# Value products of two quads in one run, and a pair of block swaps issued from ScalarE

## The chip, the cores and the metric

One core of one Trainium2 chip runs the whole kernel. The metric is the device time of one execution in microseconds; the kernel before takes 577.23 us, the median of three runs (576.55 to 578.54). TensorE multiplies, VectorE, ScalarE and GpSimd do the elementwise work, SyncE issues DMA transfers from a queue that it works off in order. In the profile the engines are called PE, DVE, ACT, POOL and SP.

## What is computed

A layer norm, a cross attention with 32 heads of width 32, an output projection and a residual, for 8 batches of 256 queries and 256 keys, in 32 bit floats; keys and values are the same context. The reference, cut to what matters:

```python
x = (hidden_states - mu) * rsqrt(var + LN_EPS) * ln_gamma + ln_beta     # (8, 256, 1024)
Q, K, V = split_heads(x @ Wq.T), split_heads(memory_keys), split_heads(memory_values)
scores = einsum('bhsd,bhtd->bhst', Q, K) * scale                        # and the mask
attn = einsum('bhst,bhtd->bhsd', softmax(scores), V)
out = residual + attn.reshape(B, S, 1024) @ Wout.T
```

## The kernel before

The work is cut into quads: four heads (128 columns) of one batch. There are 8 batches of NQ = 8 quads, N = 64 quads in all. A loop over slots n = 0 to 63 writes the program out in the order in which every engine will run it; nothing is reordered later. A slot n on TensorE holds

- `scores(n + 1)` (L486): 8 products with 32 contraction rows, 16 matmuls in the trace because a 32 bit product takes two, into four PSUM tiles;
- `values(n - 2)` (L629): the probabilities of quad n-2 times its values. 32 products, 64 matmuls in the trace, each with 64 contraction rows and 32 output columns; they go to two PSUM tiles `pv`;
- wide products, 128 by 128: steps of the output projection of the batch before (L715, a Strassen scheme with the products A11, A12, S2, S3, A22, S1, S4 and sums S1 to S4 of its operands), and a query product of the next batch but one (L345 in the first batches, L447 later).

Meanwhile `softmax(n + 1)` runs on the other engines. For each of four heads j: VectorE adds the mask and takes the minimum (`exps`, L522), ScalarE exponentiates and sums (L526), VectorE takes a reciprocal (L533), GpSimd scales (`normalize`, L535), VectorE transposes blocks of 32 by 32 into the tile `pT` (`blocks`, L541). Between the exponentials of head 0 and head 1 stands `copy_at`, in which ScalarE copies every finished `pv` out of PSUM (L642).

`pT` has halves 0 and 1 on each of four groups of 32 partitions, and the block transposes leave two of them in the wrong place. They are swapped by DMA. ScalarE first copies half 1 aside into `pc` (`aside`, L547, two calls). Then the first pair of swaps (L607) writes half 0 of the odd groups over half 1 of the even groups, and the second pair (L611) brings the even groups' old half 1, out of `pc`, into half 0 of the odd groups. The second pair therefore waits until the first has landed.

All these transfers go through SyncE's queue. For a slot n it holds, in this order: output stores that stand among the softmax work (L758), the load of the values of quad n (`load_v`, L144, two buffers, so it also waits for the products of quad n-2), the first swaps of quad n+1, loads for later (`between`: keys L136, a weight ring L414, residual L151, input L130), the second swaps of quad n+1, and after the softmax the moves of the transposed input of a later batch (`move_x`, L332), 4 in slot 4 of a batch, 6 in slot 5 and 6 in slot 6, for most batches.

`copy_at` writes into the tiles `at`: one for each half batch, three buffers. The first copy of quad 8b+4 takes the buffer of the first half of batch b-1, which is read for the last time by that batch's sum S1, an addition on GpSimd (`sum_at`, L691).

Of the kernel before, what the change touches and what calls it, by code (L numbers as in the profile page):

```python
# [46 lines left out]
F32 = mybir.dt.float32  # L47
# [4 lines left out]
P = 128  # L52
# [7 lines left out]
def xattn_kernel(  # L60
# [11 lines left out]
    nc = tc.nc  # L72
    B, S, D = x.shape
# [3 lines left out]
    NQ = NC  # L77
    NH = P // HD
    NS = S // P
    NT = T // P  # L80
    NO = D // 512
    K = 32
# [4 lines left out]
    N = B * NQ  # L87
# [16 lines left out]
    ps_v = ctx.enter_context(tc.tile_pool(name="ps_v", bufs=2, space=PS))  # L104
# [366 lines left out]
    mbs, scs, pTs, pvs, ats, pos = {}, {}, {}, {}, {}, {}  # L471
# [21 lines left out]
            pass  # L493

    tails = []


    def softmax_parts(n, copies=(), ahead=(), between=(), hooks={}, fill=()):

        fill = list(fill)

        def fill_in():
            if fill:
                fill.pop(0)()

        pss = scs[n]  # L510
        pT = pTs[n] = ptp.tile([P, 2, NI, NH, NS, K], F32, tag="pT", name=f"pT_{n}")
        pc = asp.tile([P, NI, NH, NS, K], F32, tag="pc", name=f"pc_{n}")
        es, mns, dens = {}, {}, {}

        def exps(j, part=range(NS)):
            if 0 in part:
                es[j] = ep.tile([P, NS, T], F32, tag="e", name=f"e_{n}_{j}")
                mns[j] = sm.tile([P, NS], F32, tag="mn", name=f"mn_{n}_{j}")
                dens[j] = sm.tile([P, NS], F32, tag="den", name=f"den_{n}_{j}")
            e, mn, den = es[j], mns[j], dens[j]  # L520
            for s in part:
                nc.vector.tensor_tensor_reduce(  # L522
                    out=e[:, s, :], in0=pss[j][:, s, :], in1=mbs[n // NQ], scale=1.0,
                    scalar=NO_SCORE, op0=ALU.add, op1=ALU.min, accum_out=mn[:, s : s + 1],
                )
                nc.scalar.activation(  # L526
                    e[:, s, :], e[:, s, :], AF.Exp, bias=mn[:, s : s + 1], scale=-1.0,
                    accum_out=den[:, s : s + 1],
                )

        def normalize(j):
            rden = sm.tile([P, NS], F32, tag="rden", name=f"rden_{n}_{j}")
            nc.vector.reciprocal(rden, dens[j])  # L533
            for s in range(NS):
                nc.gpsimd.tensor_scalar(  # L535
                    es[j][:, s, :], es[j][:, s, :], rden[:, s : s + 1], 1.0,
                    ALU.mult, ALU.mult,
                )

        def blocks(j):  # L540
            nc.vector.transpose(  # L541
                pT[:, :, :, j, :, :].rearrange("p a i s k -> p (a i) s k"),
                es[j].rearrange("p s (b t) -> p b s t", t=K),
            )

        def aside(j):
            nc.scalar.copy(pc[:, :, ts(j, 2)], pT[:, 1, :, ts(j, 2)])  # L547

        if n == 0:
            for j in range(NH - 1):  # L550
                exps(j, (0,))
            yield
            exps(NH - 1, (0,))
            fill_in()
            yield
            for j in range(NH):
                exps(j, (1,))
            normalize(0)
            fill_in()
        else:  # L560
            exps(0)
            while tails:
                tails.pop()()
            late = "p1" in hooks
            if not late:
                for done in list(pvs):
                    copy_at(done)
            exps(1)
            for hook in hooks.get("soon", ()):
                hook()  # L570
            exps(2)
            normalize(0)
            for hook in hooks.get("p1", ()):
                hook()
            exps(3)
            if late:
                for done in list(pvs):
                    copy_at(done)
        if n <= NQ:
            for copy in copies:  # L580
                copy()
        for hook in hooks.get(0, ()):
            hook()
        normalize(1)
        fill_in()
        blocks(0)
        for hook in hooks.get(1, ()):
            hook()
        normalize(2)
        fill_in()  # L590
        blocks(1)
        aside(0)
        normalize(3)
        fill_in()
        blocks(2)
        while fill:
            fill_in()
        if n > NQ:
            for copy in copies:
                copy()  # L600

        def tail():
            blocks(3)
            aside(1)

            for r in range(2):
                nc.sync.dma_start(pT[ts(2 * r, K), 1], pT[ts(2 * r + 1, K), 0])  # L607
            for load in between:
                load()
            for r in range(2):  # L610
                nc.sync.dma_start(pT[ts(2 * r + 1, K), 0], pc[ts(2 * r, K)])  # L611

        for load in ahead:
            load()
        if n < NQ or N - NQ < n < N - 1:
            tails.append(tail)
        else:
            tail()
        yield

    def values(n):
        pvs[n] = [
            ps_v.tile([P, 2, NS, K], F32, tag="pv", name=f"pv_{n}_{r}") for r in range(2)
        ]
        pT = pTs.pop(n)
        for i in range(NI):
            for j in range(NH):
                for r in range(2):
                    nc.tensor.matmul(  # L629
                        pvs[n][r][j * HD : (j + 1) * HD],  # L630
                        vs[n][ts(r, 2 * K), i, ts(j, HD)],
                        pT[ts(r, 2 * K), :, i, j, :, :],
                        start=(i == 0), stop=(i == NI - 1),
                    )

    def copy_at(n):
        b, c = divmod(n, NQ)
        k, c = divmod(c, NK)
        if c == 0:
            ats[b, k] = atp.tile([P, NK, NS, NA, K], F32, tag="at", name=f"at_{b}_{k}")  # L640
        for r, pv in enumerate(pvs.pop(n)):
            nc.scalar.copy(  # L642
                ats[b, k][:, c, :, ts(r, 2), :], pv.rearrange("p a s k -> p s a k")
            )
# [39 lines left out]
    def sum_at(b, name, c=slice(0, NK)):  # L684
        if name == "S2" and c.start == 0:
            s2s[b] = up.tile([P, NK, P], F32, tag="s2", name=f"s2_{b}")
        one, two, op = {
            "S3": ("A11", "A21", ALU.subtract), "S2": ("A22", "S3", ALU.subtract),
            "S1": ("S2", "A11", ALU.add), "S4": ("A12", "S2", ALU.subtract),
        }[name]  # L690
        nc.gpsimd.tensor_tensor(  # L691
            operand(b, name)[:, c], operand(b, one)[:, c], operand(b, two)[:, c], op
        )
# [213 lines left out]
    for b in range(B - 1):  # L907
        done, ends = 0, b == B - 2
        for i, counts in enumerate(steps_of(b)):
            n = NQ * (b + 1) + i  # L910
# [12 lines left out]
            product_steps(*one)  # L923


    for n in range(N):
        b, i = divmod(n - NQ, NQ)
        new_q = new_qs[n]
# [23 lines left out]
        for what, one, *args in evacuations[n]:  # L952
            if one == B - 2:
                now.append(partial(what, one, *args))
            else:
# [1 line left out]
                if one not in P1_ASIDE and i in (1, 2):  # L957
                    place = "p1" if what is keep_p1 else "soon"
                hooks.setdefault(place, []).append(partial(what, one, *args))
        if n >= 2:  # L960
            values(n - 2)
        project_steps(n, 1)
        copies = [partial(copy_q, q) for q in new_q]
# [43 lines left out]
            if n == slot:  # L1007
                sum_at(one, "S3")
        if b >= 0:
            for name in {2: ("S4",), 3 if b == B - 2 else 5: ("S1",)}.get(i, ()):  # L1010
                sum_at(b, name)
            if i == 0 and b == B - 2:
                sum_at(b, "S2", slice(0, NK - 1))
# [44 lines left out]
    for c in range(2):  # L1058
        end_steps(to_c11, "A12", B21, (c,), (0,))
        end_steps(to_c21, "A22", T4, (c,), (0,))  # L1060
    values(N - 2)
    copy_at(N - 2)
    end_sum(slice(2, 3), nc.gpsimd)
# [3 lines left out]
    s2t2 = ps_o.tile([P, 512], F32, tag="po", name="po_end_s2")  # L1067
    end_steps(s2t2, "S2", T2, range(2), (0,))
    values(N - 1)
    copy_at(N - 1)  # L1070
    end_sum(slice(3, 4), nc.vector)
# [66 lines left out]
```

## Time and profile before

| | us |
|---|---|
| median of three runs | 577.23 |
| lowest, highest | 576.55, 578.54 |
| span of the profiled execution | 577.0 |
| TensorE matmuls busy | 567.3 |
| VectorE busy | 460.4 |
| ScalarE busy | 411.7 |
| GpSimd busy | 409.8 |

The span goes from the first to the last instruction of one profiled execution. Busy time counts overlapping instructions once; matmuls are pipelined and their ends are modelled, so the distance from start to start says more than a length. SyncE has no busy time, since it only issues. In a row of the timeline stand start, length, engine, line, operation, tiles, shape and count, and in brackets the idle time of the engine before it with what ended it. "SPq" and "ACTq" are issues of a DMA; the length is that of the issue, and the landing is told in other views.

### The profile page before, as it was taken

What the parts mean: (1) busy time and instruction counts of PE and PEld (TensorE: products, weight loads), DVE (VectorE), ACT (ScalarE), POOL (GpSimd) and SP (SyncE); (2) the same over time, 40 slices, a digit from 0 to 9 for tenths busy, and PEclk for the clock granted to TensorE, in tenths of its full rate; (3) what the DMA queues carried; (4) which work ended last, traced back from release to release, by engine and by line L of the source; (5) the groups of instructions that cost most, each with busy time, mean ns of one, the idle gap of its engine ahead of it and who ended that gap; (6) DMA issues with size and microseconds to landing.
All of it is one profiled execution on the core that took longest, in us unless ns stands there. A gap on an engine that the chain in (4) does not pass through costs nothing. (4 is left out here: it accounts for less than half of the span.)

```text
span 577.0 us, 20128 instructions
## 1 busy us (share of the span) xinstructions
PE 567.3 (98%) x7162; PEld 394.2 (68%) x7162; DVE 460.4 (80%) x1695; ACT 411.7 (71%) x1425; POOL 409.8 (71%) x677
## 2 busy tenths in 40 slices
PE   8999998999999999999999999999999999999997
PEld 8788784667667777677676677667766767755543
DVE  5888887788877879979888788988878878779823
ACT  4697886677667877688677867768767776769810
POOL 1778898889896896876568675676658657448770
PEclk9999999899999999999999999999999999999999
DMA  8974766656677777957678856687567864446751
GB/s 304 394 206 126 208 161 180 192 148 166 185 220 222 200 208 207 271 166 201 188 213 228 211 138 189 212 240 206 148 161 236 224 170 130 130 138 178 199 166 73
DMA packets 50100, 111.69 MB, mean 194 GB/s; under 512 B 9424, under 2 KB 10192, under 8 KB 50000
## 3 DMA queue, kind: packets, MB, share of 16 engines
q1 hardware_dynamic: 49712, 110.40, 66.8%
q8 instruction: 57, 0.93, 0.7%
q14 instruction: 43, 0.35, 0.2%
q10 hardware_dynamic: 288, 0.01, 0.0%
HBM read 60.04 MB, written 10.49 MB: 122 GB/s over the span
## 5 line engine op out<-in xcount | busy, mean ns | idle before, releaser
L535 POOL TENSOR_SCALAR e<-e,rden 128x256 f32<-128x256 f32 x512 | 236.0, 478 | 116.9 <-DVE rden L533 114.4
L526 ACT ACTIVATE e<-e,mn 128x256 f32<-128x256 f32 x512 | 253.9, 501 | 50.7 <-DVE mn L522 49.6
L541 DVE STREAM_TRANSPOSE pT<-e 128x512 f32<-128x512 f32 x256 | 180.9, 707 | 44.7 <-POOL e L535 32.7
L522 DVE CUSTOM_DVE_ANT_0 e<-sc,mb 128x256 f32<-128x256 f32 x512 | 185.4, 416 | 26.4 <-PE sc L486 26.0
L547 ACT COPY pc<-pT 128x512 f32<-128x512 f32 x128 | 79.0, 617 | 72.1 <-DVE pT L541 36.6
L526 ACT ACTIVATION_READ_ACCUMULATOR e<-e,mn 128x1 f32 x512 | 97.9, 191 | 0.0
L345 PE MATMUL pq<-xnT,wq 128*128 128x256 f32 (+1 forms) x368 | 84.1, 383 | 0.6 <-ACT qa L354 0.6
L345 PEld LDWEIGHTS pq<-xnT,wq 128*128 128x128 f32 x368 | 68.9, 190 | 15.4 <-issue 3.7
L629 PE MATMUL pv<-pT,v 64*32 64x128 f32 x4096 | 74.7, 274 | 3.5 <-DMA v<-in_kv_dram 2.9
L629 PEld LDWEIGHTS pv<-pT,v 64*32 64x32 f32 x4096 | 57.5, 105 | 26.7 <-issue 14.7
L486 PEld LDWEIGHTS sc<-k,qa 32*128 32x128 f32 x1024 | 46.2, 184 | 41.9 <-issue 23.6
L715 PE MATMUL po_S<-wo,at 128*128 128x512 f32 x152 | 74.3, 606 | 0.0
L486 PE MATMUL sc<-k,qa 32*128 32x256 f32 x1024 | 73.6, 401 | 0.1
L715 PE MATMUL po_A<-wo,at 128*128 128x512 f32 x128 | 61.2, 620 | 0.3 <-ACT qa L354 0.3
L715 PE MATMUL po_S<-wo,s 128*128 128x512 f32 x104 | 49.9, 606 | 0.0
L533 DVE RECIPROCAL rden<-den 128x2 f32<-128x2 f32 x256 | 37.6, 147 | 7.7 <-ACT e L526 6.8
L522 DVE DVE_READ_ACCUMULATOR2_ANT mn<- 128x1 f32 x512 | 42.5, 83 | 0.0
L715 PEld LDWEIGHTS po_A<-wo,at 128*128 128x128 f32 x128 | 23.4, 193 | 26.2 <-issue 24.5
L447 PEld LDWEIGHTS pq_A<-xnT,wq 128*128 128x128 f32 x320 | 37.3, 192 | 4.8 <-issue 3.6
L715 PEld LDWEIGHTS po_S<-wo,at 128*128 128x128 f32 x152 | 25.8, 190 | 19.7 <-issue 19.1
L447 PE MATMUL pq_A<-xnT,wq 128*128 128x128 f32 x320 | 37.3, 275 | 0.0
L748 POOL TENSOR_TENSOR r<-r,p 128x512 f32<-128x512 f32 x23 | 29.4, 1278 | 7.1 <-DMA r<-in_x_dram 3.3
(96 smaller groups left out, 608.7 us busy)
## 6 DMA issues: line engine op xcount, KB each, us to landing
v<-in_kv_dram SPq DMA_DIRECT2D x64, 256.0 KB, 3.9
pT<-pT SPq DMA_DIRECT2D x128, 128.0 KB, 3.1
pT<-pc SPq DMA_DIRECT2D x128, 128.0 KB, 3.5
ring<-kept_T SPq DMA_DIRECT2D x18, 512.0 KB, 5.2
k<-in_kv_dram SPq DMA_DIRECT2D x32, 256.0 KB, 3.1
x<-in_x_dram SPq DMA_DIRECT2D x14, 512.0 KB, 5.1
r<-in_x_dram SPq DMA_DIRECT2D x28, 256.0 KB, 5.1
out_dram<-r SPq DMA_DIRECT2D x28, 256.0 KB, 3.0
```

Source lines behind the costliest of these rows:

```text
L345: nc.tensor.matmul(pqs[n], wq[:, o, c, :], xnTs[b](c), start=(c == 0), stop=(c == NC - 1),)
L447: nc.tensor.matmul(pqs[b][:, o, :], w[:, c], x_[:, c], start=begins and o + c == 0, stop=c == NK - 1, skip_group_check=True,)
L486: nc.tensor.matmul(scs[n][j][:, s, :], qa[r, n % NQ, ts(s, P)], ks[n - n % 2][r, n % 2, :], start=True, stop=True,)
L522: nc.vector.tensor_tensor_reduce(out=e[:, s, :], in0=pss[j][:, s, :], in1=mbs[n // NQ], scale=1.0, scalar=NO_SCORE, op0=ALU.add, op1=ALU.m ...
L526: nc.scalar.activation(e[:, s, :], e[:, s, :], AF.Exp, bias=mn[:, s : s + 1], scale=-1.0, accum_out=den[:, s : s + 1],)
L533: nc.vector.reciprocal(rden, dens[j])
L535: nc.gpsimd.tensor_scalar(es[j][:, s, :], es[j][:, s, :], rden[:, s : s + 1], 1.0, ALU.mult, ALU.mult,)
L541: nc.vector.transpose(pT[:, :, :, j, :, :].rearrange("p a i s k -> p (a i) s k"), es[j].rearrange("p s (b t) -> p b s t", t=K),)
L547: nc.scalar.copy(pc[:, :, ts(j, 2)], pT[:, 1, :, ts(j, 2)])
L629: nc.tensor.matmul(pvs[n][r][j * HD : (j + 1) * HD], vs[n][ts(r, 2 * K), i, ts(j, HD)], pT[ts(r, 2 * K), :, i, j, :, :], start=(i == 0), s ...
L715: nc.tensor.matmul(po, operand(b, name)[:, c], wo[:, which, c], start=begins and c == 0, stop=c == NK - 1, skip_group_check=not begins,)
L748: nc.gpsimd.tensor_tensor(r, r, p1s[b], ALU.add)
```

## The change

Three things change.

1. `values_pair(n)` writes the value products of quads n and n+1 one behind the other, into two PSUM tiles that hold both quads. The slots in `PAIRS`, odd ones from 11 to 55 without those of residue 1 modulo 8, call it for quads n-2 and n-1; the slot behind a paired one has no value products. The two quads' copies then both stand in the paired slot's softmax.
2. In the softmax of quads 10 to 56 the first pair of block swaps is issued by ScalarE, behind its second copy aside, and no longer by SyncE. The second pair stays where it was.
3. The sum S1 of a batch moves from slot 5 to slot 4 of the following batch (not in the last ones, where it is in slot 3 as before).

```diff
+    BY_ACT = range(NQ + 2, N - NQ + 1)
...
+            queue = nc.scalar if n in BY_ACT else nc.sync
             for r in range(2):
-                nc.sync.dma_start(pT[ts(2 * r, K), 1], pT[ts(2 * r + 1, K), 0])
+                queue.dma_start(pT[ts(2 * r, K), 1], pT[ts(2 * r + 1, K), 0])
...
-    def values(n):
-        pvs[n] = [
+    def values_pair(n):
+        both = [
+            ps_v.tile([P, 2, 2, NS, K], F32, tag="pv", name=f"pv_{n}_{r}") for r in range(2)
+        ]
+        for i in range(2):
+            values(n + i, [tile_[:, i] for tile_ in both])
+
+    def values(n, to=None):
+        pvs[n] = to or [
             ps_v.tile([P, 2, NS, K], F32, tag="pv", name=f"pv_{n}_{r}") for r in range(2)
         ]
...
+    PAIRS = [n for n in range(NQ + 3, N - NQ, 2) if n % NQ != 1]
+
...
-        if n >= 2:
+        if n in PAIRS:
+            values_pair(n - 2)
+        elif n >= 2 and n - 1 not in PAIRS:
             values(n - 2)
...
-            for name in {2: ("S4",), 3 if b == B - 2 else 5: ("S1",)}.get(i, ()):
+            for name in {2: ("S4",), 3 if b == B - 2 else 4: ("S1",)}.get(i, ()):
```

## The prediction

> **What bounds the kernel now.** I read the page first, then the stages, then the timeline engine by engine.
>
> ```profile
> span 577.0 us, 20128 instructions
> PE 567.3 (98%) x7162; PEld 394.2 (68%) x7162; DVE 460.4 (80%) x1695; ACT 411.7 (71%) x1425; POOL 409.8 (71%) x677
> 233.05:300.98 67.93, 67.93 (x922) 48.06 (x921) 58.22 (x213) 51.30 (x179) 46.00 (x81) 1.00 0.73 205
> ```
>
> The third line is one batch in the middle (eight slots) from the view by stages; its columns are length, PE, PEld, DVE, ACT, POOL, granted clock, DMA share and GB/s. TensorE has no idle there, so a microsecond less of TensorE work is a microsecond of time, and a stall of TensorE is lost in full. The other engines have room, but each serves the quads one after another, so their latency counts. The span of 577.0 us stands at the median of the runs, 577.23 us; sums are made on 577.0.
>
> TensorE's order in a slot n is: scores of quad n+1, value products of quad n-2, then wide products. One slot, from the timeline (start, length of the merged row):
>
> ```profile
> 249.93 1.15 PE L486 MATMUL sc<-k,qa 32*128 32x256 f32 x16
> 251.00 0.89 PEld L629 LDWEIGHTS pv<-pT,v 64*32 64x32 f32 x64 [0.33 <-issue]
> 251.01 1.16 PE L629 MATMUL pv<-pT,v 64*32 64x128 f32 x64
> 252.09 1.98 PE L715 MATMUL po_S<-wo,s 128*128 128x512 f32 x4
> ```
>
> Start to start, scores take 1.08 us and a run of values 1.08 us. The 64 weight loads of the run fill only 0.89 us, at 14 ns each; the other 0.19 us is the change of tile shape behind the run.
>
> **Part 1: values in pairs.** The list of odd slots comes out with 18 entries, residues 3, 5 and 7 of each batch of 8. An odd slot gets 128 matmuls of one shape, the even slot behind it none. Saved is one shape change per pair: 18 x 0.19 = 3.4 us. In the even slot, wide products now follow the scores directly. Early in the trace that pair of shapes stands too:
>
> ```profile
> 22.55 1.15 PE L486 MATMUL sc<-k,qa 32*128 32x256 f32 x16
> 23.62 1.14 PE L345 MATMUL pq<-xnT,wq 128*128 128x257 f32 x4
> ```
>
> Scores before wide products take the same 1.07 us, so the saving is not given back there. **Term: -3.4 us** (bounds -3.4 and 0).
>
> What the pairing asks for: the values of an even quad n run in slot n+1 and no longer in slot n+2. Its value tile v and its four block swaps must land about 7.6 us sooner. The load of v is issued in slot n, on the sync queue, behind everything queued before it. For quad 30 (scores at 267.80) the queue did this:
>
> ```profile
> 276.77 1.14 SPq L607 DMA_DIRECT2D pT<-pT  x2
> 277.96 0.58 SPq L130 DMA_DIRECT2D x<-in_x_dram  x1
> 279.10 1.14 SPq L611 DMA_DIRECT2D pT<-pc  x2
> 280.29 4.41 SPq L332 DMA_DIRECT2D xnT<-xe  x6
> 284.80 0.53 SPq L758 DMA_DIRECT2D out_dram<-r  x1
> 285.42 0.41 SPq L144 DMA_DIRECT2D v<-in_kv_dram  x1
> v<-in_kv_dram SPq DMA_DIRECT2D x64, 256.0 KB, 3.9
> ```
>
> The last line is from the page: a v load lands 3.9 us (median) after issue, so this one lands at 285.42 + 3.9 = 289.3. The order of these entries is the same after the change, except that the first swaps leave the queue. They were not late here, and the second swaps (L611) wait for their landing whoever issued them; then come six moves at 0.7 us each, an output store, and only then v. When is it wanted? Slot 31 begins with its scores:
>
> ```profile
> 284.82 1.15 PE L486 MATMUL sc<-k,qa 32*128 32x256 f32 x16
> 145.56 1.15 PE L486 MATMUL sc<-k,qa 32*128 32x256 f32 x16
> 147.00 0.40 SPq L144 DMA_DIRECT2D v<-in_kv_dram  x1
> 421.70 1.15 PE L486 MATMUL sc<-k,qa 32*128 32x256 f32 x16
> 423.40 0.41 SPq L144 DMA_DIRECT2D v<-in_kv_dram  x1
> ```
>
> The second run of a pair begins 1.08 + 0.89 = 1.97 us behind the scores; and the slot itself begins 0.2 us sooner (the pair slot before it 0.89 longer, the even one 1.08 shorter). Quad 30: 284.82 + 1.97 - 0.2 = 286.6, short by 2.7 us. The other pairs of rows are the first and the last of the five quads with six moves ahead of v (14, 22, 30, 38, 46): 147.00 + 3.9 = 150.9 against 147.3, short by 3.6; and 427.3 against 423.5, short by 3.8. Mean 3.4. **Term: five times 3.4 = +17 us.** Nothing hides it: the next instructions of TensorE are queued behind these values. ScalarE's copies of both value tiles stand between the first and second head's exponentials and wait for the whole pair, so the next softmax is held for as long and gains no lead. Bounds: from above 5 x 3.8 = 19 us; from below the quickest landings, of v 2.8 us in this answer for its line and of the swaps 1.1 us under their median (part 2), which leave 5 x (3.4 - 1.1 - 1.1) = 6 us.
>
> ```profile
> L144 SPq DMA_DIRECT2D v<-in_kv_dram x48: 376/532/1725, 97.8 to 496.1; - x48
> DMA to landing us min/median/max: 2.8/4.0/6.8
> ```
>
>
> The quads of residue 2 (10, 18, 26, 34, 42, 50) are paired in slots 11 to 51; the first and the last of the six:
>
> ```profile
> 109.08 0.41 SPq L144 DMA_DIRECT2D v<-in_kv_dram  x1
> 109.43 1.15 PE L486 MATMUL sc<-k,qa 32*128 32x256 f32 x16
> 454.34 0.40 SPq L144 DMA_DIRECT2D v<-in_kv_dram  x1
> 454.74 1.15 PE L486 MATMUL sc<-k,qa 32*128 32x256 f32 x16
> ```
>
> Short by 109.08 + 3.9 - 109.43 - 1.97 = 1.6 us and by 1.5. Some of these lie behind a queue that the change relieves, so I take two thirds of 6 x 1.55: **+6 us** (bounds 0 and 9). Residue 4:
>
> ```profile
> 266.07 0.53 SPq L144 DMA_DIRECT2D v<-in_kv_dram  x1
> 267.80 1.15 PE L486 MATMUL sc<-k,qa 32*128 32x256 f32 x16
> ```
>
> 269.97 against 269.57: at the edge. I take 0 (bounds 0 and 6 x 0.4 = 2.4).
>
> **Part 2: two swaps on ScalarE.** Neither an issue between computing instructions of ScalarE nor its own price there stands in the trace; the nearest rows are its two issues at the start and the pair on the sync queue, 1.14 above.
>
> ```profile
> 0.72 0.41 ACTq L195 DMA_DIRECT2D gam<-in_gamma_dram  x1
> 1.16 0.45 ACTq L196 DMA_DIRECT2D bet<-in_beta_dram  x1
> 268.06 0.64 ACT L547 COPY pc<-pT 128x512 f32<-128x512 f32 x1
> 269.56 0.51 ACT L526 ACTIVATE e<-e,mn 128x256 f32<-128x256 f32 x1 [0.86 <-DVE mn L522]
> 252.12 1.24 ACT L252 ACTIVATE x<-x,shift,rstd 128x1024 f32<-128x1024 f32 x1
> ```
>
> So 0.9 to 1.14 us per quad; I take 1.1, since these are the same transfers. They wait for the copy aside and stand ahead of the next quad's exponentials. ScalarE idled 0.86 us at that point, so 0.25 us shows in an ordinary slot. Behind an even slot, whose successor's scores come 1.08 us sooner, up to 1.3 us shows; and where a normalization (the 1.24 us row, two per batch) stands there, all 1.1. What is late next: the exponentials, the last transpose, the swaps, and v behind them. I take 0.5 us on each of the eleven late loads: **+5.5 us** (bounds 0 and 11 x 1.1 = 12).
>
> The gain it could bring is an earlier landing of the first swaps:
>
> ```profile
> L607 SPq DMA_DIRECT2D pT<-pT x96: 507/582/1892, 98.4 to 499.6; - x96
> DMA to landing us min/median/max: 2.2/3.3/5.6
> ```
>
> For quad 30 the second swaps went out at 279.10, 2.3 us behind the first swaps' issue: nothing is left to win there. [...]
>
> **Part 3: the sum S1** goes from slot 5 of a batch to slot 4 on GpSimd, because the copies of the pair reach the buffer that it frees one slot sooner. It is the same addition beside the same softmax work, a slot in which GpSimd then has two, and the next slot one: 0 (bounds 0 and one addition, 1.3 us by the row of its like below, in six batches = 8, if it came late for those copies).
>
> ```profile
> 251.02 1.29 POOL L691 TENSOR_TENSOR at<-at,s 128x512 f32<-128x512 f32 x1
> ```
>
> **What a stall sets off.** In the one place where the values already waited for v, the clock fell:
>
> ```profile
> 101.18 1.25 PE L629 MATMUL pv<-pT,v 64*32 64x128 f32 x64 [2.05 <-DMA v<-in_kv_dram]
> 102.36 3.68 PE L715 MATMUL po_A<-wo,at 128*128 128x512 f32 x4
> 102.48:105.88 3.40, 3.40 (x5) 1.34 (x6) 2.75 (x17) 3.03 (x13) 3.39 (x4) 0.50 0.81 216
> ```
>
> After 2.05 us of waiting, 3.4 us ran at clock 0.50, which costs 1.7 us. The five long stalls are longer than that one; I take three such falls: **+5 us** (bounds 0 and 5 x 1.7 = 8.5). [...]
>
> Sum: 577.0 - 3.4 + 17 + 6 + 5.5 + 5 = **607 us**.
>
> **Rivals.**
> - *ScalarE paces the batch, and the loads come in time.* From the first exponential (269.56) to the end of the copy aside (the swap issue at 276.77) a quad takes 7.2 us; with 1.1 behind it 8.3, eight of them plus two normalizations 68.9 us, against 67.93 - 3 x 0.19 = 67.4 for TensorE. The batch would be 1.0 us longer than now, 5.75 batches: 583 us. With the short stalls of the lower bound (6) it is 589. For it: swaps that overtake the sync queue. Against it: six moves and the store stay ahead of v. It decides where 8.3 us passes the mean slot.
> - *Faster:* the loads come in time and ScalarE's slack covers the issues: 577 - 3.4 = 573.6. For it: TensorE alone is full today. Against it: the walk of quad 30.
> - *Worse:* full clock falls (8.5), issue delay (12), late residues 2 and 4 (9 + 2.4) and 19 for the five: 577 - 3.4 + 50 = 624.
> - *The pairing does nothing* (no shape change saved) and nothing stalls: 577.
>
> **How the numbers follow.** Late loads as summed, 595 to 620: 0.55. ScalarE or short stalls, 580 to 595: 0.22. Worse, over 620: 0.10. Faster: 0.09. No change: 0.04. A measurement of this kernel tells some 0.3% (1.7 us) from none. Predicted 607; the range 585 to 624 leaves out faster and no change (0.13), a little of the ScalarE case and the far end (0.07 together). Slower 0.87, same 0.04, faster 0.09.
>
> **What would show it.** In slots 15, 23, 31, 39 and 47 a wait of values for v or for the swaps of 3 us or more, each; some 2 us or less in slots of residue 3; runs of 128 value matmuls with no gap elsewhere, 0.9 us longer than 64; clock 0.50 behind the long waits; the first exponential 0.3 to 1.3 us later behind its scores. Wrong it would be if the v loads of even quads leave the sync queue 3 us earlier than they did, or if TensorE stays without idle through a batch.

## The result and the profile after

The changed kernel takes 638.47 us, the median of four runs (635.44 to 639.66), against 577.1 us for the kernel before on the same chip (four runs, 576.55 to 578.54). The ratio is 1.1045, with a 95% interval of 1.1007 to 1.1084. The forecast was 607, with a range up to 624: the sign was right, and the time lies above the range. In the experiments below, runs more than 1.5% above the fastest run of the same kernel are left out of the times. (In the code after, the values are at L638, the first swaps at L609, the second at L613, the exponentials at L527, the copy aside at L548, the projection's steps at L724, the output store at L767; the other lines named here have kept their numbers.)

First the page of the kernel after:

```profile
span 637.3 us, 19999 instructions
PE 584.5 (92%) x7162; PEld 403.5 (63%) x7162; DVE 462.3 (73%) x1695; ACT 413.3 (65%) x1425; POOL 410.2 (64%) x677
```

The span grew by 60.3 us. TensorE's busy time grew by 584.5 - 567.3 = 17.2, its idle time from 577.0 - 567.3 = 9.7 to 637.3 - 584.5 = 52.8, by 43.1. The other engines do the same work as before in a longer time. So there are two questions: what did TensorE wait for, and why was it busy for longer with the same 7162 matmuls? The view of the waits answers the first (line, releaser, total us, times, longest):

```profile
PE pv L638 <- DMA v<-in_kv_dram: 23.7, 9, 4.7
PE pv L638 <- issue: 16.0, 6, 7.0
PE po_S L724 <- DVE r L766: 5.1, 8, 1.3
PE po_S L724 <- issue: 1.6, 1, 1.6
```

Waits in front of value products make up 23.7 + 16.0 = 39.7 us. In the kernel before the same view had

```profile
PE pv L629 <- DMA v<-in_kv_dram: 2.9, 2, 2.1
PE pv L629 <- DMA pT<-pT: 0.5, 1, 0.5
```

so 36.3 us are new. "issue" is the name the view gives where it sees no releaser; for the longest of these, 7.0 us, the timelines below show a load of v landing there. The last two rows, 6.7 us, are projection steps that wait for VectorE to empty their PSUM tile. 36.3 + 6.7 = 43.0 is the whole new idle time.

The view by stretches answers the second. The columns are the stretch and its length, the busy times of PE, PEld, DVE, ACT and POOL, the granted clock, the DMA share and GB/s. The first row is the batch of quads 26 to 33, which took 67.93 before; the others are the stretches at half clock.

```profile
255.33:335.28 79.95, 70.24 (x921) 49.38 (x921) 58.53 (x212) 51.68 (x180) 46.04 (x81) 0.96 0.63 176
...
111.50:118.20 6.70, 5.68 (x69) 3.27 (x70) 2.17 (x13) 5.58 (x20) 2.10 (x3) 0.50 0.66 190
155.90:162.50 6.60, 5.51 (x70) 3.84 (x71) 1.70 (x7) 3.36 (x15) 1.52 (x4) 0.50 0.90 229
237.80:244.40 6.60, 5.95 (x76) 4.54 (x77) 2.06 (x7) 3.70 (x16) 1.73 (x5) 0.50 0.54 143
316.30:323.00 6.70, 3.28 (x66) 2.41 (x67) 0.00 (x0) 1.13 (x6) 0.00 (x0) 0.50 0.93 239
398.30:401.50 3.20, 3.20 (x66) 2.23 (x64) 0.00 (x0) 1.28 (x7) 0.00 (x0) 0.50 0.92 276
476.80:480.00 3.20, 3.20 (x61) 1.93 (x44) 0.00 (x0) 1.62 (x8) 0.00 (x0) 0.50 0.45 104
514.30:517.50 3.20, 3.20 (x66) 2.29 (x65) 0.90 (x5) 1.56 (x9) 0.93 (x2) 0.50 0.85 258
```

In these seven rows, which are cut up to 0.2 us inside the stretches, TensorE was busy at half clock for 30.0 us; half of that, 15.0, is lost, against 1.7 before: 13 us more. That leaves 17.2 - 13 = some 4 us of the busy time, and the 2.5 us that the pairing saves besides, that no row of these views names.

Now quad 30, the one that the prediction walked through. On the sync queue and on ScalarE (start, length of the issue):

```profile
302.40 0.58 SPq L144 DMA_DIRECT2D v<-in_kv_dram  x1
303.03 0.47 SPq L130 DMA_DIRECT2D x<-in_x_dram  x1
309.05 1.15 SPq L613 DMA_DIRECT2D pT<-pc  x2
310.25 3.99 SPq L332 DMA_DIRECT2D xnT<-xe  x6
314.34 0.54 SPq L767 DMA_DIRECT2D out_dram<-r  x1
314.97 0.40 SPq L144 DMA_DIRECT2D v<-in_kv_dram  x1
```

```profile
303.62 1.16 ACTq L609 DMA_DIRECT2D pT<-pT  x2
```

And on TensorE, the paired slot 31 with its wait, and a pair without one two slots earlier:

```profile
293.72 2.10 PE L638 MATMUL pv<-pT,v 64*32 64x128 f32 x128
295.75 1.12 PE L724 MATMUL po_S<-wo,at 128*128 128x512 f32 x2
...
310.33 1.26 PE L486 MATMUL sc<-k,qa 32*128 32x256 f32 x16
311.53 1.16 PE L638 MATMUL pv<-pT,v 64*32 64x128 f32 x64
319.72 2.08 PE L638 MATMUL pv<-pT,v 64*32 64x128 f32 x64 [7.04 <-issue]
```

The load of v goes out at 314.97, behind second swaps, six moves and a store, as forecast. It lands at 319.63 by the transfer's record, and the second run of the pair starts at 319.72, after 7.04 us of idle where 2.7 were forecast. The rest of the slip stands in the rows ahead: the second swaps left 309.05 - 303.62 = 5.4 us after the first swaps' issue, where before it was 2.3. The x load, formerly behind the first swaps, now stood right ahead of them; that it made the difference is likely, but no run was made for it.

In the pair without a wait, 2.03 us pass from the start of the values to the start of the projection step; one run alone takes 1.09. So a second run costs 0.94 and saves 1.09 in the next slot: about 0.14 us per pair, not 0.19.

### The profile page after: what moved, and what is told of

The parts are those of the page before. It is cut to its first block, busy times and chain, and to the rows that moved or that the text cites. A ratio compares the mean times of both kernels' runs of the same rounds, so it can differ in the third digit from the quotient of the medians.

```text
span 637.3 us, 19999 instructions
## 1 busy us (share of the span) xinstructions
PE 584.5 (92%) x7162; PEld 403.5 (63%) x7162; DVE 462.3 (73%) x1695; ACT 413.3 (65%) x1425; POOL 410.2 (64%) x677
## 4 chain that ended last, share of the span: by engine, by line
PE 38%; POOL 17%; DVE 13%; ACT 11%; DMA 11%; issue 6%; ACTq 3%; SPq 2%; DVEq 0%; POOLq 0%
POOL e L536 13%; PE po_S L724 8%; PE pq L345 6%; ACT e L527 6%; PE pq_A L447 5%; PE pv L638 5%; DVE pT L542 5%; PE sc L486 4%; DMA v<-in_kv_dram 4%; DVE e L523 4%; DMA pT<-pT 3%; ACTq L609 3%; PE po_A L724 3%; PE po_end L791 2%; ACT pc L548 2%
## 5 line engine op out<-in xcount | busy, mean ns | idle before, releaser
L527 ACT ACTIVATE e<-e,mn 128x256 f32<-128x256 f32 x512 | 253.6, 501 | 70.0 <-DVE mn L523 53.4
L548 ACT COPY pc<-pT 128x512 f32<-128x512 f32 x128 | 79.0, 618 | 70.1 <-DVE pT L542 37.4
L638 PE MATMUL pv<-pT,v 64*32 64x128 f32 x4096 | 80.9, 289 | 39.9 <-DMA v<-in_kv_dram 23.7
L638 PEld LDWEIGHTS pv<-pT,v 64*32 64x32 f32 x4096 | 63.5, 111 | 60.7 <-issue 44.7
L527 ACT ACTIVATION_READ_ACCUMULATOR e<-e,mn 128x1 f32 x512 | 98.2, 192 | 0.0
L724 PE MATMUL po_S<-wo,at 128*128 128x512 f32 x152 | 74.3, 606 | 0.0
L486 PEld LDWEIGHTS sc<-k,qa 32*128 32x128 f32 x1024 | 45.7, 184 | 43.1 <-issue 26.1
L724 PE MATMUL po_S<-wo,s 128*128 128x512 f32 x104 | 57.7, 685 | 6.8 <-DVE r L766 5.1
L724 PE MATMUL po_A<-wo,at 128*128 128x512 f32 x128 | 59.5, 605 | 0.3 <-ACT qa L354 0.3
L651 ACT COPY at<-pv 128x128 f32<-128x128 f32 x128 | 25.0, 262 | 35.0 <-PE pv L638 35.0
L724 PEld LDWEIGHTS po_S<-wo,at 128*128 128x128 f32 x152 | 25.8, 190 | 21.4 <-issue 20.9
L724 PEld LDWEIGHTS po_A<-wo,at 128*128 128x128 f32 x128 | 22.9, 189 | 25.7 <-issue 24.0
L724 PEld LDWEIGHTS po_S<-wo,s 128*128 128x128 f32 x104 | 19.9, 212 | 27.7 <-issue 20.5
```

The lines of the kernel that those rows point to most:

```text
L486: nc.tensor.matmul(scs[n][j][:, s, :], qa[r, n % NQ, ts(s, P)], ks[n - n % 2][r, n % 2, :], start=True, stop=True,)
L527: nc.scalar.activation(e[:, s, :], e[:, s, :], AF.Exp, bias=mn[:, s : s + 1], scale=-1.0, accum_out=den[:, s : s + 1],)
L638: nc.tensor.matmul(pvs[n][r][j * HD : (j + 1) * HD], vs[n][ts(r, 2 * K), i, ts(j, HD)], pT[ts(r, 2 * K), :, i, j, :, :], start=(i == 0), s ...
L651: nc.scalar.copy(ats[b, k][:, c, :, ts(r, 2), :], pv.rearrange("p a s k -> p s a k"))
L724: nc.tensor.matmul(po, operand(b, name)[:, c], wo[:, which, c], start=begins and c == 0, stop=c == NK - 1, skip_group_check=not begins,)
```

## The experiments

The theory behind the first experiments was that of the prediction: late loads of v in the paired slots make up most of the loss, and the issues on ScalarE matter only through them. The rival was that ScalarE's issues lengthen the softmax by themselves and pace the batch.

**Pairs alone.** The change with all swaps on the sync queue.

```diff
-    BY_ACT = range(NQ + 2, N - NQ + 1)
+    BY_ACT = ()
```

> The changed kernel with all first swaps back on SyncE; pairs and the moved sum S1 stay. Theory (late loads): the loads of v still stand behind the second swaps and the moves, so the pairs wait: 17 us in slots of residue 7, up to 9 in residue 3, some 12 of half clock behind them, 2.5 saved: 605 to 615 us. Rival (ScalarE's issues are the main cost): pairs alone cost little, under 590 us.

Measured: 610.34 us (609.81 to 615.26), ratio 1.0603 (1.0556 to 1.0651). The page's span and TensorE row, then the view of the waits:

```profile
span 608.5 us, 20095 instructions
PE 577.4 (95%) x7162; PEld 401.1 (66%) x7162; DVE 458.5 (75%) x1695; ACT 413.5 (68%) x1425; POOL 411.3 (68%) x677
```

```profile
PE pv L638 <- issue: 16.0, 8, 3.5
PE pv L638 <- DMA v<-in_kv_dram: 9.0, 5, 3.8
...
PE pv L638 <- DMA pT<-pT: 1.0, 1, 1.0
```

Waits for values are 26.0 us, 22.6 more than before. By slots, from starts of scores, 16.8 of it stands in the five slots of residue 7 and 6.2 in those of residue 3. No projection step waits for VectorE. TensorE was busy at half clock in five stretches (three of 3.4 us, two of 6.8), which costs 9.2 us more than before. With the 2.5 us that 18 pairs save, that makes 577.0 + 22.6 + 9.2 - 2.5 = 606, 2 us short of the span. So the late loads are real, and their waits have the forecast size (22.6 us against 17 + 6). Pairs alone cost 610.3 us against 576.1 of the kernel before beside them: 34 of the 61 us, and no more.

**Swaps alone.** The kernel before with the first swaps of quads 10 to 56 issued by ScalarE.

```diff
+            queue = nc.scalar if n in BY_ACT else nc.sync
...
-                nc.sync.dma_start(pT[ts(2 * r, K), 1], pT[ts(2 * r + 1, K), 0])
+                queue.dma_start(pT[ts(2 * r, K), 1], pT[ts(2 * r + 1, K), 0])
```

> The kernel before with the first swaps of quads 10 to 56 issued by ScalarE, nothing else. Theory (late loads): values are wanted two slots behind their softmax as before, ScalarE's 1.16 us per quad still fit into the mean slot of 8.4 us: 577 to 584 us and no wait for v. Rival (ScalarE's issues): 600 us or more.

Measured: 601.5 us (599.37 to 603.35), ratio 1.043 (1.0393 to 1.0467); the span is 597.4. This is where the forecast fell: 25 us more than the 576.1 of the kernel before beside it, with no pair in the kernel. The view by stretches for the batch of quads 26 to 33, the waits of TensorE, and one end of a softmax on ScalarE (the next quad's first exponential is the last row):

```profile
237.61:312.67 75.06, 69.27 (x922) 48.28 (x921) 58.05 (x210) 50.27 (x174) 45.27 (x79) 1.00 0.66 182
```

```profile
PE po_S L717 <- DVE r L759: 12.9, 13, 2.6
```

```profile
362.34 0.62 ACT L548 COPY pc<-pT 128x512 f32<-128x512 f32 x1 [1.56 <-DVE pT L542]
362.99 1.16 ACTq L609 DMA_DIRECT2D pT<-pT  x2
364.25 0.51 ACT L527 ACTIVATE e<-e,mn 128x256 f32<-128x256 f32 x1 [1.29 <-DVE mn L523]
```

The clock stays at 1.00 and only some 3 us of waits stand in front of value products, as before. Instead the batch takes 75.06 us, 7.1 more (it is the one hit hardest; the six batches from quad 10 on are 21.3 us longer together, by the starts of their scores), and TensorE waits for VectorE's evacuation of the projection, which VectorE does among its softmax work. The exponential starts 0.10 us behind the end of the issue; the wait for `mn` in its bracket counts the issue as idle time, since issues are not counted as work. So the issue stood in the way.

Whether TensorE or the softmax sets the pace shows in another row of the waits: VectorE, which opens a softmax by adding the mask to the scores, waits for TensorE's scores. The first row is of the kernel before, the second of swaps alone:

```profile
DVE e L522 <- PE sc L486: 26.0, 28, 2.1
DVE e L523 <- PE sc L486: 5.8, 12, 1.5
```

Before, the softmax waited for TensorE for 26.0 us; now it hardly does (5.8 us), and TensorE waits for the softmax's engines.

The place of the loss shows in the loop that a softmax forms. The table gives means over quads 10 to 55, from the starts and ends of ScalarE's rows: the body, from a quad's first exponential to the end of its copy aside; the gap from there to the next quad's first exponential; and their sum.

| kernel | body | gap | loop |
|---|---|---|---|
| before | 7.63 | 1.03 | 8.65 |
| pairs alone | 8.34 | 0.99 | 9.33 |
| swaps alone | 7.25 | 1.88 | 9.13 |
| filler on ScalarE (below) | 7.30 | 1.69 | 8.99 |
| after | 8.22 | 1.76 | 9.98 |

Before, the loop is as long as TensorE's slot, because TensorE sets it: the body is stretched by waiting. With the issues the body shrinks to 7.25, its least here, and body and gap together still come to 9.13. That is 0.48 us more than a slot, in 46 quads 22 us. This sum is the lost time told again, since the loops of the quads add up to the time that they take; what the table adds is where it went: the gap grew by 0.85 and the body could give up only 0.38 of it. With the turn of the waits above, the softmax loop has become the bound, most of all where the slots were shortest. In the kernels with pairs the body is long again, because quads wait for late values: ScalarE's copies out of `pv` (L642 before, L651 after) wait 33.8 us with pairs alone and 35.0 after, against 8.9 before.

**Time on ScalarE without any issue.** The kernel before, with two copies of `pc` onto itself behind the copy aside of quads 10 to 56.

```diff
             aside(1)
+            if NQ + 2 <= n <= N - NQ:
+                nc.scalar.copy(pc, pc)
+                nc.scalar.copy(pc[:, :1], pc[:, :1])
```

> The kernel before, all swaps on SyncE, with two copies of a tile onto itself (1024 and 256 elements per partition, together about 1.35 us) on ScalarE where the changed kernel issues the swaps. Theory (ScalarE's time in the softmax chain): as long as the issues, so the time is that of the run with the swaps alone, 595 to 605 us. Rival (the transfers: a second queue, loads that run ahead of the swaps and share the engines): no transfer changes its queue here, 577 to 582 us.

Measured: 593.6 us (593.23 to 594.28), ratio 1.0291 (1.0258 to 1.0323). The two copies in the view by lines (count, busy time, mean ns of one, idle before):

```profile
L606 ACT COPY pc<-pc 128x1024 f32<-128x1024 f32 x47 | 49.2, 1047 | 1.5
L607 ACT COPY pc<-pc 128x256 f32<-128x256 f32 x47 | 19.0, 405 | 1.5
```

1.45 us of plain work at that place costs 17 us in all (576.5 for the kernel before beside it), just under the range expected. The softmax hardly waits for TensorE's scores here either, 5.7 us against 26.0. So time in that chain, with no transfer moved to another queue, explains about two thirds of the 25 us. Between the two medians 601.5 - 593.6 = 8 us remain, between the two profiled spans 597.4 - 592.5 = 4.9. It is not that ScalarE is held longer on average: from the end of the copy aside to the end of the last added instruction 1.52 us pass in both kernels, by the rows of ScalarE for the 47 quads. But the copies always take 1.51 to 1.52 us, while with the issues 1.19 to 4.08 us pass, more than 1.5 in 13 quads. What the trace of swaps alone shows of them (ns min/median/max; first and last start):

```profile
L609 ACTq DMA_DIRECT2D pT<-pT x94: 513/528/1854, 101.0 to 521.0; - x94
L609 ACTq EVENT_SEMAPHORE  x47: 17/17/2800, 100.4 to 519.8; - x47
```

Single issues took up to 1.85 us, and ScalarE once stood for 2.80 us at the semaphore in front of a pair. The first swaps also land later: the pages give a median of 4.6 us after the issue for those from ScalarE, and 2.7 for all first swaps in the kernel with the copies. Which of the two, the uneven times or the later landing, makes up the 8 us is not shown.

**Loads behind the second swaps.** Swaps alone, with the `between` loads queued behind the second swaps, so that no load stands right ahead of the swaps.

```diff
-            for load in between:
-                load()
...
             for r in range(2):
                 nc.sync.dma_start(pT[ts(2 * r + 1, K), 0], pc[ts(2 * r, K)])
+            for load in between:
+                load()
```

> The kernel with the swaps alone on ScalarE, but with the loads for later behind the second swaps on SyncE's queue, so that they no longer run ahead of the swaps and share the engines with them. Theory (ScalarE's time in the softmax chain): no change, 598 to 604 us. Rival (the shared DMA engines make the 8 us by which the swaps cost more than the copies of the same length): 590 to 595 us.

Measured: 611.2 us (two runs, 609.25 and 613.13), ratio 1.0594 (1.0544 to 1.0644): 10 us slower than swaps alone, which neither theory had. Its profiled execution took 622.78 us, so its rows are not used. The edit also holds every such load until the first swaps have landed, so it does not isolate the order. Inconclusive; the 8 us stay open.

**v early.** In a paired slot both loads, of quads n and n+1, go ahead of the swaps, once with the swaps on ScalarE as after, once with pairs alone.

```diff
-        ahead = [partial(load_v, n)] if n > 1 else []
+        ahead = [partial(load_v, n)] if n > 1 and n - 1 not in PAIRS else []
+        if n in PAIRS:
+            ahead.append(partial(load_v, n + 1))
```

> The changed kernel, but a paired slot issues the loads of v of both quads whose buffers it frees (n and n+1), so the load of an even quad leaves a slot sooner, ahead of the moves; swaps stay on ScalarE. Theory (late loads): residues 4 and 6 wait for the second swaps at most, 1 us or less, the half clock behind residue 7 is gone; residue 2 (the load still late, because its buffer comes free in the slot before) waits as now, 11 us and some half clock: 595 to 605 us. Rival: the time stays near 638.

> Both: pairs, loads of v a slot sooner, and first swaps back on SyncE. Theory (late loads): only residue 2 waits, 6 to 9 us, with one or two half clocks; 2.5 saved: 580 to 590 us. Rival (ScalarE's issues): the same as without early loads, under 590 too; told apart by the first run of this set.

Measured: 619.4 us (614.25 to 621.91), ratio 1.0697 (1.0632 to 1.0762), with the swaps on ScalarE; 588.7 us (two runs, 587.5 and 589.87), ratio 1.0209 (1.0164 to 1.0253), with pairs alone. On the sync queue of the second kernel, in the slot of the same quad 30 (this profiled execution took 597.07 us; what is read from it is the order of the queue):

```profile
283.41 1.08 SPq L144 DMA_DIRECT2D v<-in_kv_dram  x2
...
289.80 1.14 SPq L613 DMA_DIRECT2D pT<-pc  x2
290.99 3.76 SPq L332 DMA_DIRECT2D xnT<-xe  x6
```

Both loads are out 6.4 us ahead of the second swaps and the moves. In the slots of residue 7 the waits fall from 26.3 to 0.3 us in the one kernel, and from 16.8 to nothing in the other: the queue order was the cause there. The second kernel lies in the range expected; waits in the slots of residue 3 stayed, as expected (9.9 us in that execution). The first is slower than expected: these waits grew with the swaps on ScalarE, to 17.3 us against 11.1. Why they grew was not tried further. With v early, the swaps on ScalarE cost 619.4 - 588.7 = 31 us (28 by the ratios); without it 638.47 - 610.34 = 28 (25 by the ratios); without pairs 25. So the two parts of the change cost nearly separate sums.

**TensorE kept at work in the wait.** The change, with 16 unused 128 by 128 products between the two runs of a pair in the slots of residue 7 from 15 to 47. Their results go to a part that is added to the value tile.

```diff
+            if i and n % NQ == 5 and n < N - NQ - 3:
+                for _ in range(16):
+                    nc.tensor.matmul(
+                        both[0][:, 2:4].rearrange("p i a s k -> p (i a s k)")[:, :P], wo[:, B11, 0, :P], wo[:, B11, 0, :P],
+                        start=True, stop=True, skip_group_check=True,
+                    )
```

> The changed kernel with 16 added products (128 by 128, about 3.5 us of TensorE, result unused) between the two value runs of the paired slots of residue 7 in slots 15 to 47. Theory (waits of over 2 us halve the clock behind them): the added work runs inside waits of 4.5 to 7.3 us, the half clock of 13.7 us in these five slots goes: 622 to 628 us. Rival (the clock falls for another reason, or the waits are not there): 638 us or up to 655.

Measured: 627.4 us (626.67 to 634.17), ratio 1.091 (1.0851 to 1.0969): 11 us less than after by the medians, 8 by the ratios. TensorE's rows in slots 15 and 39 (the unused products are 32 matmuls in the trace), and the stretches behind them:

```profile
151.08 3.84 PE L630 MATMUL pv<-wo 128*128 128x128 f32 x32
158.76 2.08 PE L644 MATMUL pv<-pT,v 64*32 64x128 f32 x64 [3.84 <-issue]
...
392.93 3.84 PE L630 MATMUL pv<-wo 128*128 128x128 f32 x32
397.75 1.25 PE L644 MATMUL pv<-pT,v 64*32 64x128 f32 x64 [0.98 <-DMA v<-in_kv_dram]
```

```profile
158.30:165.00 6.70, 6.24 (x72) 4.40 (x73) 2.18 (x6) 3.73 (x17) 1.51 (x4) 0.50 0.66 175
398.00:402.00 4.00, 4.00 (x85) 3.32 (x79) 1.06 (x3) 2.96 (x13) 0.91 (x2) 1.00 0.90 245
```

In slots 31, 39 and 47 no more than 1.63 us of waiting remain and the clock stays at 1.00; in 15 and 23 waits of 3.84 and 2.75 us remain and it falls (in 23 the two projection products behind the values took 2.08 us, in 31 1.12). So in these five slots the half clock went with the longer waits, and it comes on top of them: the values took 2.08 us in slot 15 and 1.25 in slot 39, both 64 matmuls.

**The sum S1 alone.** The kernel before with S1 in slot 4.

```diff
-            for name in {2: ("S4",), 3 if b == B - 2 else 5: ("S1",)}.get(i, ()):
+            for name in {2: ("S4",), 3 if b == B - 2 else 4: ("S1",)}.get(i, ()):
```

> The kernel before with the sum S1 in slot 4 instead of 5, nothing else. Theory: nothing, 576 to 578 us. Rival (GpSimd's added 1.3 us delays the softmax of slot 5): 580 to 585 us.

Measured: 576.67 against 576.47, ratio 0.9999 (0.9974 to 1.0023). It cost nothing that can be measured.

**Is there a version that gains?** Pairs alone with v early, and only those pairs whose loads can come in time: ten pairs, then nine of them.

```diff
-    PAIRS = [n for n in range(NQ + 3, N - NQ, 2) if n % NQ != 1]
+    PAIRS = [n for n in range(NQ + 5, N - NQ - 1, 2) if n % NQ > 3 and n not in (21, 23)]
```

> Pairs only in ten slots (13, 15, 23, 29, 31, 37, 39, 45, 47, 53), where the early loads of v left no wait, swaps on SyncE. Theory (late loads): ten shape changes saved at 0.14 us, 1.4 us, less what the even quad of the first pair of a batch still waits, 0 to 2 us: 574 to 578 us. Rival: pairing costs elsewhere (the sum S1, the copies), over 580 us.

> The kernel with few pairs without slot 23 as well, whose even quad 22 had no paired slot before it and so still loaded its v behind the moves: nine pairs (13, 15, 29, 31, 37, 39, 45, 47, 53). Theory (late loads): no wait is left but 0.4 us in slot 13, nine shape changes saved, 1.3 us: 574 to 577 us, ratio 0.995 to 1.000. Rival: what made the run before 6 us slower is something else than slot 23: 580 us or more.

Measured: with ten pairs (only 21 left out) 582.68 us (579.52 to 584.44), ratio 1.0104 (1.0074 to 1.0134). One slot spoils it, 23: slot 21 is not paired, so v of quad 22 is not loaded early.

```profile
218.58 1.96 PE L638 MATMUL pv<-pT,v 64*32 64x128 f32 x64 [3.38 <-DMA v<-in_kv_dram]
```

That one wait, with 6.8 us at half clock behind it, made the slot 7.3 us longer, 0.9 of it for the second run itself. With nine pairs 575.23 us (twelve runs) against 577.42 (seventeen), ratio 0.9984 (0.9963 to 1.0006). A batch in the middle has no idle left:

```profile
230.00:298.00 68.00, 67.98 (x924) 48.31 (x920) 57.16 (x211) 51.64 (x179) 45.15 (x80) 1.00 0.74 208
```

Nine pairs at 0.14 us would save 1.3 us, 0.2%. The interval holds that and holds no change too. No version was found that certainly beats the kernel before.

## Why the prediction was right or wrong

**The saved shape change (-3.4).** Right in kind. A pair saves 0.14 us, not 0.19, 2.5 us in all: of the 0.19 us from the end of the weight loads to the next start, which the prediction put down to the change of shape, 0.05 is not saved.

**Late v in residues 7 and 2 (+17 and +6).** Right for pairs alone, which show 16.8 and 6.2 in the slots named (residue 2 is paired in slots of residue 3); loading v ahead of the moves takes the 16.8 away. The 6.2 came otherwise than told: 3.1 us in slot 11, 1.4 in 35, 1.8 in 51 and none in the other three, where six quads were to be late by some 1.5 us each; that the sum agrees is in part luck. The upper bound of 3.8 us a quad was read from the first and last of five; by the same sum quad 38, whose v left 3.0 us after the scores of slot 39 in the kernel before, was 5.2 short. In the whole change the same slots show 26.3 and 11.1. In the five of residue 7 v left 12.5 us after the scores in sum, against 8.4 with pairs alone, two thirds of the difference in slot 31; and it landed 4.3 to 5.4 us after its issue (four of the five have a record), against 2.9 to 4.5. Why it landed later was not tried.

**Residue 4 (0) and S1 (0).** Right: pairs alone have 1.0 us in the slots of residue 5, and S1 alone has a ratio of 0.9999.

**Part 2, the swaps on ScalarE (+5.5).** This step failed. The price of a pair of issues was about right (1.1 forecast; 1.16 in the row above, 1.3 on average, 1.5 with the waits in front of it in swaps alone), but the prediction let it reach the end only through eleven late loads, at 0.5 us each ("I take 0.5 us on each of the eleven late loads"). In the runs it reaches the end with no late load at all, spread over the quads. Of 1.3 us, 0.85 shows in the mean gap (1.03 to 1.88; this mean holds the quads with a normalization and the long issues too), where 0.25 us in an ordinary slot was forecast. Body and gap then take 9.13 us, longer than the slot of 8.65, and on average a quad pays the difference: 25 us by the medians, where the term had an upper bound of 12. Plain work in the same place, which cost 17 us, shows that most of it is ScalarE's time in that chain.

**The rival "ScalarE paces the batch".** It named this mechanism, at 68.9 us a batch. It was short for the same reason: its 8.6 us a quad (8.3 and a share of two normalizations) held 1.1 us for the gap besides them, and 7.25 + 1.88 = 9.13 is what the runs showed. And it stood as an alternative to late loads, where it was an addition: 34 us for pairs alone and 25 for swaps alone make 59 of the 61.

**The clock (+5).** Right in kind, too small. Three falls of 3.4 us were taken; pairs alone have five stretches, two of them twice as long, 9 us; the whole change has seven, four of them twice as long, 13 us.

**The landing of the first swaps.** Nothing was to be won at quad 30, by the prediction, and nothing was: there the second swaps left 3.1 us later behind the first than before. That quad is the extreme, though: on average over quads 10 to 56 the second swaps left 3.73 us behind the first, against 3.45 before. Issued by ScalarE, the first swaps had a median landing, from issue, of 3.4 us after and 4.6 with swaps alone, against 3.3 from SyncE before. In neither did the queue of their own bring them in sooner.

What remains open: 8 us that issues on ScalarE cost beyond plain work of the same length, some 4 us of TensorE's busy time in the whole change (swaps alone has 3.5 more too, 570.8 on its page, with the clock at 1.00, so the clock need not be the cause), why v landed later in the whole change, and why waits in residue 3 grew with v early.

## What to carry to other kernels

Before work is put into the idle time of an engine that is not the bound, add up the serial loop that the engine belongs to, with the new work in it, and compare the sum with the slot of the engine that sets the pace. When two mechanisms speak against a change, ask whether they exclude each other; here they added up. A work order that consumes a buffer a slot sooner has to be checked against the queue order of its load, and where TensorE stalled here, the clock was a second price beside the wait: 13 us beside 36.3 in the whole change, 9.2 beside 22.6 in pairs alone.

## What the hardware showed beside this

The seven stretches at half clock in the kernel after stand, in order of time, at waits of value products of 3.63, 4.69, 4.20, 7.04, 4.70, 4.42 and 2.06 us. The first four took 6.8 us, the last three 3.4, and the longer wait did not always go with the longer stretch: 3.63 us came with 6.8, 4.70 us with 3.4. A wait of 1.97 us in slot 27 left the clock at 1.00. Slot 31 in five stretches:

```profile
309.38:312.79 3.41, 3.30 (x83) 1.70 (x81) 3.12 (x10) 1.24 (x2) 2.27 (x4) 1.00 0.51 118
312.79:316.21 3.42, 0.00 (x0) 0.00 (x0) 2.15 (x13) 1.09 (x4) 0.93 (x2) 1.00 0.80 232
316.21:319.62 3.41, 0.00 (x0) 0.00 (x0) 0.00 (x0) 0.00 (x0) 0.00 (x0) 0.50 0.92 234
319.62:323.03 3.41, 3.31 (x66) 2.44 (x67) 0.00 (x0) 1.16 (x7) 0.00 (x0) 0.50 0.93 240
323.03:326.45 3.42, 3.42 (x29) 3.16 (x29) 2.28 (x7) 3.07 (x13) 2.00 (x5) 0.99 0.20 63
```

TensorE idles from 312.68 to 319.72. In this slot the clock is still 1.00 in the second row, which holds 3.42 us of the wait, 0.50 in the rest of it, still 0.50 while TensorE works for 3.31 of the next 3.41 us, and 0.99 only after that. What decides when the clock falls and for how long is not shown: this was read from one trace, and no experiment was made for it.
